# Mask lanes and the first norm in PSUM, two more gathered tiles split into one-pass halves, and 24 row buffers

## The chip, the cores and the metric

The kernel runs on one core of a Trainium2 chip. The metric is the device time of one execution in microseconds (us); lower is better. Times of runs are medians of several executions.

## The reference

Two graph layers over 10,000 nodes of 512 float32 features, and 160,000 edges sorted by destination. What is computed:

```
h   = relu(layernorm(x))
msg = (h @ rel_W[type])[src]                      # one of 4 products for each edge
agg = segment_sum(msg, dst) / max(degree, 1)
x1  = layernorm(h + h @ self_W + agg) * ln1_w + ln1_b
f   = gelu(x1 @ W1 + b1) @ W2 + b2
x   = x + layernorm(x1 + f) * ln2_w + ln2_b
h1  = relu(layernorm(x))
h2  = relu(h1 @ W_self1 + mean_of_neighbours(h1) @ W_neigh1 + b1)
out = x + relu(h2 @ W_self2 + mean_of_neighbours(h2) @ W_neigh2 + b2)
```

## The kernel before

Nodes are handled in 79 blocks: 78 of 128 rows and one of 16, which comes first. The program has four stages: (1) the first norm of the input, the four relation products of every node (written to `hall_d` in DRAM) and the building of edge lists; (2) the fused stage, which gathers and sums messages, and does both layer norms and the feed-forward part; (3) and (4) the two neighbour layers, which gather rows of `h_d`. The change touches stage 2, and through a shared function the order of matmuls in stages 3 and 4.

**Gathering.** `gather` issues indirect DMAs on POOL, each for a tile of 128 rows of 512 floats (L844). A full block has 11 tiles of its own rows (`row`), in which row p of each tile belongs to node p, so that DVE adds them straight into PSUM (`add`, L908). It has five tiles of other edges (`orow`), which PE sums with a 0/1 mask as the stationary operand (`sums`, L897). One more tile is shared by 4 blocks and one by 16 blocks (`srow`). Row tiles come from a ring of buffers, 28 in stage 2 and 56 later, in order of allocation: a gather waits until the last reader of its slot is done.

**Splitting.** In stage 2 the shared tiles are split by `halves_of`: DVE masks off the low 12 bits into `top` (L834, a row tile of the ring), DVE writes the rest to `lower` (L836), and ACT copies `top` to `upper` (L837). Both halves are of type float32r[...].

**Masks.** `hots` builds a block's masks of 128 x 7 x 128 by comparing `lane` with `loc` on DVE (L870). In stages 3 and 4 ACT builds them.

**One iteration of stage 2** handles block b. Instructions of each engine run in program order:

1. DVE builds the mask of block b+1 (L870). In two of four iterations it also adds the feed-forward results of two earlier blocks to their rests and takes their statistics (`second`, L1092, L1063, L1064).
2. DVE adds the block's 11 tiles to PSUM (L908), scales by degree and adds the self product (L1176), and takes statistics.
3. PE runs a part of an earlier group's feed-forward work (`products`): four up products of four matmuls each, with a gelu on ACT after each, or two down products of eight matmuls. A group has four blocks, so the parts go up, up, down, down. One block is turned (transposed) in the middle of a part.
4. ACT takes the square root of the variances, DVE the reciprocal (L1072), and `scaled` applies the norms: ACT scales, DVE multiplies by the weight and adds (L1117, L1118 for the first norm, L1122, L1123 for the second).
5. `begin` gathers for block b+1, splits a shared tile where one starts, and issues the mask matmuls. `products` has issued its last call on PE before them.

The first iterations also multiply 24 late blocks by `self_W`; these pass through tiles of the same ring (`fetch`, `residuals`).

Of the kernel before, what the change touches and what calls it, by code (L numbers as in the profile page):

```python
# [16 lines left out]
P = 128  # L17
# [4 lines left out]
def kernel(  # L22
# [789 lines left out]
    def aligned(ctxa):  # L812

        psA = ctxa.enter_context(tc.tile_pool(name="psA", bufs=2, space=PSUM))
        ring = []
        RINGS = (28, 56)
        UPPER = -(1 << 12)
        rest = list(range(full))
        blocks = ([full] if N % P else []) + rest

# [6 lines left out]
            pool, n = ring[-1]  # L827
            return pool.tile([P, D], F32, name="rows", bufs=n)

        def halves_of(v, lv, pool):  # L830

            top = row_tile()
            hi, lo = (pool.tile([P, D], F32, name=f"{k}{lv}", bufs=1) for k in ("upper", "lower"))
            nc.vector.tensor_scalar(top.bitcast(I32), v.bitcast(I32), UPPER, None,  # L834
                                    op0=OP.bitwise_and)
            nc.vector.tensor_tensor(lo.bitcast(F32R), v, top, op=OP.subtract)  # L836
            nc.scalar.copy(hi.bitcast(F32R), top)  # L837
            return hi, lo

        def gather(b, table, pool, split):  # L840

            def rows(n, idx, name=None, bufs=None):
                t = pool.tile([P, D], F32, name=name, bufs=bufs) if name else row_tile()
                nc.gpsimd.indirect_dma_start(  # L844
                    out=t[:n], out_offset=None, in_=table,
                    in_offset=bass.IndirectOffsetOnAxis(ap=idx, axis=0))
                return t[:n]

            for lv, n in enumerate(SPANS):
                if b < full and b % n == 0:  # L850
                    idx = srow[lv][:, b // n:b // n + 1]
                    if split:
                        tails[lv] = halves_of(rows(P, idx), lv, pool)
                    else:
                        tails[lv] = rows(P, idx, f"tail{lv}", 2)
            others = [rows(P, orow[:, b, t:t + 1]) for t in range(OT if b < full else OT_LAST)]
            if b < full:
                others += tails
            return others, [rows(P, row[:, b, t:t + 1]) for t in range(own(b))]

        def hots(b, pool, scalar=False):
            n = OT + NL if b < full else OT_LAST
            hot = pool.tile([P, OT + NL, P], F32, name="hot", bufs=2)
            if scalar:
# [5 lines left out]
            nc.vector.tensor_tensor(hot[:, :n].bitcast(F32R),  # L870
                                    lane[:, None, :].to_broadcast([P, n, P]),
                                    loc[:, b, :n].unsqueeze(2).to_broadcast([P, n, P]),
                                    op=OP.is_equal)
            return hot
# [6 lines left out]
        def sums(b, others, hot, idle=None):  # L881

            r, n = height(b), len(others)
            pa = psA.tile([P, D], F32, name="pa")
            if idle:
                keep_busy(pa, *idle)
            order = list(range(n)) if b == full else list(range(OT, n))[::-1] + list(range(OT))
            work = []
            for t in order:
                if isinstance(others[t], tuple):  # L890
                    work += [(hot[:, t, :r].bitcast(F32R), v.bitcast(F32R)) for v in others[t]]
                else:
                    work.append((hot[:, t, :r], others[t]))
            if len(work) > n and b % SPANS[0] == 0:
                work = work[-OT:] + work[:-OT]
            for i, (h, v) in enumerate(work):
                nc.tensor.matmul(pa[:r], h, v, start=(i == 0), stop=(i == len(work) - 1))  # L897
            return pa
# [12 lines left out]
        with ExitStack() as s:  # L911
# [1 line left out]
            wp = s.enter_context(tc.tile_pool(name="wp2", bufs=1))  # L913
            gp = s.enter_context(tc.tile_pool(name="gp", bufs=1))
            sp = s.enter_context(tc.tile_pool(name="sp", bufs=3))
            psT = s.enter_context(tc.tile_pool(name="psT2", bufs=2, space=PSUM))
            psH = s.enter_context(tc.tile_pool(name="psH", bufs=2, space=PSUM))
            psO = s.enter_context(tc.tile_pool(name="psO", bufs=2, space=PSUM))
            w1s = wp.tile([P, KC, F], F32, name="w1s")
# [62 lines left out]
            fetch(LATE[0])  # L982
            for b in blocks[:2]:
                load(b)
            first_hot = hots(blocks[0], gp)
# [63 lines left out]
            class Scales:  # L1049
# [27 lines left out]
                def apply(self, out, v, c, r, func):  # L1077
                    nc.scalar.activation(out, v, func, bias=self.rs[:r, 1, c:c + 1],
                                         scale=self.rs[:r, 0, c:c + 1])

            rests = {}
            fed, third = [], []
            now = Scales()
# [13 lines left out]
            def scaled(got, first):  # L1097

                nonlocal third, now
                if first:  # L1100
                    b, c = first
                    r, v = height(b), nodes[b]
                    now.apply(v[:r], v[:r], c, r, AF.Identity)
                if third:
                    h1, at = pair(h1_d, third[0][0], len(third), "h1", 2)
                    for k, (b, c) in enumerate(third):
                        now.apply(h1[:, k, :], xrs.pop(b), c, height(b), AF.Relu)
                    nc.sync.dma_start(at, h1)
                third = []
                for b, v, c in got:  # L1110
                    r = height(b)
                    now.apply(v[:r], v[:r], c, r, AF.Identity)
                if first:
                    b, c = first
                    r, v = height(b), nodes[b]
                    rests[b] = gp.tile([P, D], F32, name="rest", bufs=11)
                    nc.vector.tensor_tensor(rests[b][:r], v[:r], ln1w[:r], op=OP.mult)  # L1117
                    nc.vector.tensor_tensor(rests[b][:r], rests[b][:r], lnb2[:r], op=OP.add)  # L1118
                now = Scales()
                for b, v, c in got:  # L1120
                    r = height(b)
                    nc.vector.tensor_tensor(v[:r], v[:r], ln2w[:r], op=OP.mult)  # L1122
                    nc.vector.tensor_tensor(xrs[b], xrs[b], v[:r], op=OP.add)  # L1123
                    third.append((b, now.stats(xrs[b], r)))
                if got:
                    b, n = got[0][0], len(got)
                    nc.sync.dma_start(rows_of(xn_d, (b, n, height(b))), xrs.pop((b, n)))
# [29 lines left out]
            for bs in plan:  # L1157
                for b in bs:
                    r = height(b)
                    if b == bs[0]:  # L1160
                        before, grp = grp, Group(bs)
                    if i + 2 < len(blocks):
                        load(blocks[i + 2])
                    if i + 1 < len(blocks):
                        hot = hots(blocks[i + 1], gp)
# [24 lines left out]
                    i += 1  # L1190
# [14 lines left out]
        for step, (h_d, ws, wn, bs) in enumerate(((h1_d, ws1, wn1, bs1), (h2_d, ws2, wn2, bs2))):  # L1205
            with ExitStack() as s:
# [45 lines left out]
                    load(i)  # L1252
                turn(blocks[0])
                before = None
                held = begin(blocks[0], hots(blocks[0], ip, True), h_d, ip)
                for i, b in enumerate(blocks):
                    r = height(b)
                    load(i + 3)
                    if i + 1 < len(blocks):
                        hot = hots(blocks[i + 1], ip, True)  # L1260
# [336 lines left out]
```

## Time and profile before

| | us |
|---|---|
| median of 3 runs (lowest to highest) | 6226.65 (6225.09 to 6230.65) |
| the profiled execution's own time | 6229.31 |
| its span, first to last instruction | 6227.6 |
| PE busy (share of the span) | 5669.9 (91%) |
| DVE busy | 3657.2 (59%) |
| ACT busy | 1858.6 (30%) |
| POOL busy | 3769.6 (61%) |
| first to last gather of stage 2 | 1208.0 to 2903.3 |
| first gather of stage 3 | 3002.2 |
| first gather of stage 4 | 4614.2 |

A line of the profile's groups names the source line, engine, operation and tiles (written <- read), the form and the count; then come the busy time in us and the mean of one in ns; then the engine's idle time just before such instructions, and what ended it. "Issue" means that the engine waited for nothing that the profile shows. A float32 matmul stands in the profile as two records.

### The profile page before, as it was taken

What the parts mean: (1) busy time and instruction counts of PE and PEld (TensorE: products, weight loads), DVE (VectorE), ACT (ScalarE), POOL (GpSimd) and SP (SyncE); (2) the same over time, 40 slices, a digit from 0 to 9 for tenths busy, and PEclk for the clock granted to TensorE, in tenths of its full rate; (3) what the DMA queues carried; (4) which work ended last, traced back from release to release, by engine and by line L of the source; (5) the groups of instructions that cost most, each with busy time, mean ns of one, the idle gap of its engine ahead of it and who ended that gap; (6) DMA issues with size and microseconds to landing.
All of it is one profiled execution on the core that took longest, in us unless ns stands there. A gap on an engine that the chain in (4) does not pass through costs nothing.

```text
span 6227.6 us, 55230 instructions
## 1 busy us (share of the span) xinstructions
PE 5669.9 (91%) x15103; PEld 2565.6 (41%) x15103; DVE 3657.2 (59%) x7447; ACT 1858.6 (30%) x3672; POOL 3769.6 (61%) x3927
## 2 busy tenths in 40 slices
PE   9999999899999999999788888888879888888888
PEld 4555554444444444444333333333334333333333
DVE  8889999457777777776333434434434444444444
ACT  1026665023333333333322222222222222222221
POOL 0001110167777777774577777777767777777776
PEclk9999999999999999999899999999999999999999
DMA  4333344487888887885677777777778888888877
GB/s 160 118 126 121 127 138 156 144 276 244 255 252 257 247 252 245 255 255 181 203 237 237 234 237 236 236 237 234 237 232 251 251 247 250 251 247 249 251 246 217
DMA packets 503502, 1373.79 MB, mean 221 GB/s; under 512 B 82206, under 2 KB 82206, under 8 KB 503054
## 3 DMA queue, kind: packets, MB, share of 16 engines
q0 software_dynamic: 308768, 1008.91, 54.4%
q1 hardware_dynamic: 193886, 360.20, 15.9%
q8 instruction: 122, 2.00, 0.1%
q14 instruction: 198, 1.62, 0.1%
q10 hardware_dynamic: 528, 1.05, 0.1%
HBM read 1156.54 MB, written 213.30 MB: 220 GB/s over the span
## 4 chain that ended last, share of the span: by engine, by line
DMA 40%; PE 37%; DVE 9%; issue 7%; POOL 5%; ACT 2%; SPq 0%; POOLq 0%; DVEq 0%; ACTq 0%
DMA rows<-h_d,row 20%; PE pm L774 15%; DMA rows<-h_d,orow 13%; PE pa L897 6%; POOL rows L844 5%; DMA rows<-hall_d,row 5%; PE po L1036 4%; DVE pa L908 4%; PE ph L1025 4%; PE pm L678 2%; PE po L1268 1%; PE po L976 1%; DMA rows<-hall_d,orow 1%; DVE st L1063 1%; PE pT L172 1%
## 5 line engine op out<-in xcount | busy, mean ns | idle before, releaser
L908 DVE TENSOR_TENSOR pa<-pa,rows 128x512 f32<-128x512 f32 x2574 | 1799.2, 699 | 2061.9 <-PE pa L897 1212.3
L844 POOL DMA_INDIRECT rows<-h_d,row x1716 | 1622.3, 945 | 522.7 <-issue 285.7
L897 PE MATMUL pa<-rows,hot 128*128 128x512 f32 (+1 forms) x2358 | 1240.4, 639 | 375.9 <-DMA rows<-h_d,orow 321.1
L844 POOL DMA_INDIRECT rows<-hall_d,row x858 | 870.1, 1014 | 268.7 <-issue 111.2
L844 POOL DMA_INDIRECT rows<-h_d,orow x786 | 743.1, 945 | 354.9 <-issue 102.0
L897 PEld LDWEIGHTS pa<-rows,hot 128*128 128x128 f32 (+1 forms) x2358 | 399.7, 192 | 1156.7 <-DMA rows<-h_d,orow 830.1
L844 POOL DMA_INDIRECT rows<-hall_d,orow x393 | 377.4, 960 | 350.5 <-PE pm L678 203.4
L1268 PE MATMUL po<-wss,hTb 128*128 128x512 f32 (+1 forms) x1264 | 588.7, 610 | 0.0
L1036 PE MATMUL po<-w2s,hid 128*128 128x512 f32 (+1 forms) x1264 | 564.4, 600 | 16.7 <-DVE rest L1092 13.5
L1239 PE MATMUL po<-wns,mTb 128*128 128x512 f32 (+1 forms) x1264 | 574.3, 597 | 1.4 <-ACT mTb L173 1.4
L1025 PE MATMUL ph<-x1T,w1s 128*128 128x512 f32 (+2 forms) x1344 | 558.9, 569 | 4.8 <-ACT hid L1027 4.8
L173 ACT COPY mTb<-pT 128x512 f32<-128x512 f32 (+1 forms) x158 | 91.9, 581 | 1231.7 <-PE pT L172 1231.7
L1264 ACT ACTIVATE mb<-pa,rdeg 128x512 f32<-128x512 f32 (+1 forms) x158 | 108.6, 687 | 1131.9 <-DVE pa L908 1128.6
L879 PE MATMUL pa<-wss,ident 128*128 128x512 f32 x936 | 427.5, 593 | 0.0
L513 POOL DMA_INDIRECT win<-rec_d,at x79 | 81.4, 1031 | 528.4 <-PE pe L538 348.0
L1239 PEld LDWEIGHTS po<-wns,mTb 128*128 128x128 f32 (+1 forms) x1264 | 240.5, 191 | 308.5 <-issue 272.8
L1025 PEld LDWEIGHTS ph<-x1T,w1s 128*128 128x128 f32 x1344 | 249.7, 192 | 282.0 <-issue 272.9
L1036 PEld LDWEIGHTS po<-w2s,hid 128*128 128x128 f32 (+1 forms) x1264 | 237.0, 191 | 306.3 <-issue 281.8
L897 PE MATMUL pa<-tail,hot 128*128 128x512 f32 x624 | 307.8, 610 | 48.9 <-DMA tail<-h_d,srow 48.7
L866 ACT ACTIVATE hot<-lane,loc 128x128 f32<-128x128 f32 x1098 | 337.7, 390 | 0.0
L1268 PEld LDWEIGHTS po<-wss,hTb 128*128 128x128 f32 (+1 forms) x1264 | 237.2, 198 | 241.4 <-issue 241.0
L774 PE MATMUL pm<-wrel,hT 128*128 128x512 f32 x624 | 296.5, 597 | 0.0
(304 smaller groups left out, 6344.3 us busy)
## 6 DMA issues: line engine op xcount, KB each, us to landing
hall_d<-p SPq DMA_DIRECT2D x156, 256.0 KB, 2.5
hall_d<-u SPq DMA_DIRECT2D x156, 256.0 KB, 2.5
hb<-h_d SPq DMA_DIRECT2D x156, 256.0 KB, 4.2
rows<-h_d,row POOLq DMA_INDIRECT x1716, 3.8
xg<-in_x_dram SPq DMA_DIRECT2D x39, 512.0 KB, 3.8
xr_d<-xg SPq DMA_DIRECT2D x39, 512.0 KB, 2.8
xs<-xs_d SPq DMA_DIRECT2D x39, 512.0 KB, 6.6
h_d<-h SPq DMA_DIRECT2D x39, 512.0 KB, 4.6
```

The lines of the kernel that those rows point to most:

```text
L678: nc.tensor.matmul(pm, a[:, k, :], w[:, k, :], start=(k == 0), stop=(k == KH - 1))
L774: nc.tensor.matmul(pm, a[:, k, :], w[:, k, :], start=(k == 0), stop=(k == KH - 1))
L844: nc.gpsimd.indirect_dma_start(out=t[:n], out_offset=None, in_=table, in_offset=bass.IndirectOffsetOnAxis(ap=idx, axis=0))
L866: nc.scalar.activation(hot[:, t, :], lane, AF.Abs, bias=loc[:, b, t:t + 1], scale=-1.0)
L879: nc.tensor.matmul(p, ident, w, start=True, stop=True)
L897: nc.tensor.matmul(pa[:r], h, v, start=(i == 0), stop=(i == len(work) - 1))
L908: nc.vector.tensor_tensor(pa[:r], pa[:r], t[:r], op=OP.add)
L1025: nc.tensor.matmul(ph[:, :n], w1s[:, k, f * P:(f + 1) * P], self.xT[:, k, :n], start=(k == 0), stop=(k == KC - 1))
L1036: nc.tensor.matmul(po[:r], self.hid[:, f, c * r:(c + 1) * r], w2s[:, f, :], start=(f == 0), stop=(f == FC - 1))
L1239: nc.tensor.matmul(po[:r], mT[:, k, :r], wns[:, k, :], start=False, stop=(k == KC - 1))
L1264: nc.scalar.activation(m[:r], pa[:r], AF.Copy, scale=rdeg[:r, b:b + 1])
L1268: nc.tensor.matmul(po[:r], hT[:, k, :r], wss[:, k, :], start=(k == 0), stop=False)
```

## The change

- `hots` in stage 2 reads the lane numbers from a PSUM copy (`lanes`), made once by ACT. Stages 3 and 4 keep their masks on ACT; the flag `scalar` becomes the absence of `lanes`.
- The block's sum stays in PSUM: the step at L1176 writes `pa` in place instead of `xs`, the statistics read `pa`, ACT's scaled copy goes from `pa` to `xs`, and the first norm's rest is made from `pa` by `affine`.
- `affine` replaces a scaling on ACT, a multiply and an add by two scalar-tensor-tensor operations on DVE: subtract the mean and multiply by the weight in place, then multiply by the reciprocal deviation and add. It is used for the first norm's rest and for the second norm. The second norm is now done before the first norm's rest.
- The first two of a block's five `orow` tiles are split by `halves_of`. Their `top` tiles come from the ring as well.
- In a full block the five `orow` tiles are multiplied from last to first, in all stages, so that the split ones come last. Where a shared tile starts, the three unsplit tiles come first, then the shared halves, then the two split tiles.
- The ring of stage 2 has 24 row tiles, not 28. The transposes have one PSUM buffer, not two; the lanes take the other bank.

```diff
-        RINGS = (28, 56)
+        RINGS = (24, 56)
+        SPLIT = 2
...
             others = [rows(P, orow[:, b, t:t + 1]) for t in range(OT if b < full else OT_LAST)]
+            if split and b < full:
+                for t in range(SPLIT):
+                    others[t] = halves_of(others[t], NL + t, pool)
...
             nc.vector.tensor_tensor(hot[:, :n].bitcast(F32R),
-                                    lane[:, None, :].to_broadcast([P, n, P]),
+                                    lanes[:, None, :].to_broadcast([P, n, P]),
...
-            order = list(range(n)) if b == full else list(range(OT, n))[::-1] + list(range(OT))
+            order = list(range(n)) if b == full else list(range(OT, n))[::-1] + list(range(OT))[::-1]
...
-            if len(work) > n and b % SPANS[0] == 0:
-                work = work[-OT:] + work[:-OT]
+            if b < full and isinstance(others[OT], tuple) and b % SPANS[0] == 0:
+                work = work[2 * NL:2 * NL + OT - SPLIT] + work[:2 * NL] + work[2 * NL + OT - SPLIT:]
...
-            psT = s.enter_context(tc.tile_pool(name="psT2", bufs=2, space=PSUM))
+            psT = s.enter_context(tc.tile_pool(name="psT2", bufs=1, space=PSUM))
+            psC = s.enter_context(tc.tile_pool(name="psC", bufs=1, space=PSUM))
...
+            lanes = psC.tile([P, D], F32, name="lanes")[:, :P]
+            nc.scalar.copy(lanes, lane)
+            first_hot = hots(blocks[0], gp, lanes)
...
+                def affine(self, out, v, c, r, w, to):
+                    nc.vector.scalar_tensor_tensor(v, v, self.mv[:r, c, 0:1], w[:r],
+                                                   op0=OP.subtract, op1=OP.mult)
+                    nc.vector.scalar_tensor_tensor(out, v, self.rs[:r, 0, c:c + 1], to,
+                                                   op0=OP.mult, op1=OP.add)
...
-                    now.apply(v[:r], v[:r], c, r, AF.Identity)
+                    now.apply(nodes[b][:r], pa[:r], c, r, AF.Identity)
...
+                last, now = now, Scales()
                 for b, v, c in got:
                     r = height(b)
-                    now.apply(v[:r], v[:r], c, r, AF.Identity)
+                    last.affine(xrs[b], v[:r], c, r, ln2w, xrs[b])
+                    third.append((b, now.stats(xrs[b], r)))
                 if first:
...
-                    nc.vector.tensor_tensor(rests[b][:r], v[:r], ln1w[:r], op=OP.mult)
-                    nc.vector.tensor_tensor(rests[b][:r], rests[b][:r], lnb2[:r], op=OP.add)
-                now = Scales()
-                for b, v, c in got:
-                    r = height(b)
-                    nc.vector.tensor_tensor(v[:r], v[:r], ln2w[:r], op=OP.mult)
-                    nc.vector.tensor_tensor(xrs[b], xrs[b], v[:r], op=OP.add)
-                    third.append((b, now.stats(xrs[b], r)))
+                    last.affine(rests[b][:r], pa[:r], c, r, ln1w, lnb2[:r])
...
-                    nc.vector.scalar_tensor_tensor(v[:r], pa[:r], rdeg[:r, b:b + 1], v[:r],
+                    nc.vector.scalar_tensor_tensor(pa[:r], pa[:r], rdeg[:r, b:b + 1], v[:r],
                                                    op0=OP.mult, op1=OP.add)
-                    first = (b, now.stats(v[:r], r))
+                    first = (b, now.stats(pa[:r], r), pa)
```

More of the change, by code (lines that the diff above doesn't have):

```diff
@@ L828, in row_tile, with halves_of @@
             return pool.tile([P, D], F32, name="rows", bufs=n)
-        def halves_of(v, lv, pool):
+        def halves_of(v, lv, pool, bufs=1):
             top = row_tile()
-            hi, lo = (pool.tile([P, D], F32, name=f"{k}{lv}", bufs=1) for k in ("upper", "lower"))
+            hi, lo = (pool.tile([P, D], F32, name=f"{k}{lv}", bufs=bufs) for k in ("upper", "lower"))
             nc.vector.tensor_scalar(top.bitcast(I32), v.bitcast(I32), UPPER, None,
@@ L859, in gather, with hots @@
             return others, [rows(P, row[:, b, t:t + 1]) for t in range(own(b))]
-        def hots(b, pool, scalar=False):
+        def hots(b, pool, lanes=None):
             n = OT + NL if b < full else OT_LAST
             hot = pool.tile([P, OT + NL, P], F32, name="hot", bufs=2)
-            if scalar:
+            if lanes is None:
                 for t in range(n):
@@ L984, in aligned @@
                 load(b)
-            first_hot = hots(blocks[0], gp)
+            lanes = psC.tile([P, D], F32, name="lanes")[:, :P]
+            nc.scalar.copy(lanes, lane)
+            first_hot = hots(blocks[0], gp, lanes)
             residuals(LATE[0])
@@ L1100, in scaled @@
                 if first:
-                    b, c = first
-                    r, v = height(b), nodes[b]
-                    now.apply(v[:r], v[:r], c, r, AF.Identity)
+                    b, c, pa = first
+                    r = height(b)
+                    now.apply(nodes[b][:r], pa[:r], c, r, AF.Identity)
                 if third:
@@ L1109, in scaled @@
                 third = []
+                last, now = now, Scales()
                 for b, v, c in got:
                     r = height(b)
-                    now.apply(v[:r], v[:r], c, r, AF.Identity)
+                    last.affine(xrs[b], v[:r], c, r, ln2w, xrs[b])
+                    third.append((b, now.stats(xrs[b], r)))
                 if first:
-                    b, c = first
-                    r, v = height(b), nodes[b]
+                    b, c, pa = first
+                    r = height(b)
                     rests[b] = gp.tile([P, D], F32, name="rest", bufs=11)
-                    nc.vector.tensor_tensor(rests[b][:r], v[:r], ln1w[:r], op=OP.mult)
-                    nc.vector.tensor_tensor(rests[b][:r], rests[b][:r], lnb2[:r], op=OP.add)
-                now = Scales()
-                for b, v, c in got:
-                    r = height(b)
-                    nc.vector.tensor_tensor(v[:r], v[:r], ln2w[:r], op=OP.mult)
-                    nc.vector.tensor_tensor(xrs[b], xrs[b], v[:r], op=OP.add)
-                    third.append((b, now.stats(xrs[b], r)))
+                    last.affine(rests[b][:r], pa[:r], c, r, ln1w, lnb2[:r])
                 if got:
@@ L1164, in aligned @@
                     if i + 1 < len(blocks):
-                        hot = hots(blocks[i + 1], gp)
+                        hot = hots(blocks[i + 1], gp, lanes)
                     ready = []
@@ L1254, in aligned @@
                 before = None
-                held = begin(blocks[0], hots(blocks[0], ip, True), h_d, ip)
+                held = begin(blocks[0], hots(blocks[0], ip), h_d, ip)
                 for i, b in enumerate(blocks):
@@ L1259, in aligned @@
                     if i + 1 < len(blocks):
-                        hot = hots(blocks[i + 1], ip, True)
+                        hot = hots(blocks[i + 1], ip)
                     pa, mine = held
```

## Prediction

> **What bounds the kernel now.** I read the page's busy shares first, then its costliest groups, then the fused stage alone. PE is busy 91% of the span and POOL only 61%, but the groups of the gathers (L844; busy us, mean ns of one, idle before) show another picture:
>
> ```profile
> L844 POOL DMA_INDIRECT rows<-h_d,row x1716 | 1622.3, 945 | 522.7 <-issue 285.7
> L844 POOL DMA_INDIRECT rows<-hall_d,row x858 | 870.1, 1014 | 268.7 <-issue 111.2
> ```
>
> 268.7 us over 858 gathers is 0.31 us before each, and so it is in the last two stages (522.7/1716 = 0.30). The timelines show this gap after nearly every gather: it is the pace of issue, not a wait. So a gather costs POOL 0.945 + 0.304 = 1.249 us, and that queue is full. Next, the steady part of the fused stage (1400 to 2900 us):
>
> ```profile
> L844 POOL DMA_INDIRECT rows<-hall_d,row x779 | 793.5, 1019 | 237.3 <-issue 100.5 <-DMA rows<-hall_d,row 40.8 <-DMA rows<-hall_d,orow 27.1
> L844 POOL DMA_INDIRECT rows<-hall_d,orow x351 | 335.9, 957 | 106.9 <-issue 30.5 <-DVE pa L908 25.6 <-DMA rows<-hall_d,row 22.5
> ```
>
> 1152 gathers with their gaps take 1149 + 351 = 1500 us of 1500: POOL bounds this stage. A block has 16.32 gathers, so 70.6 blocks pass, 21.25 us each: 16.32 x 1.249 = 20.38, and 0.88 of lengthening ((1019-945) x 779 + (957-945) x 351 = 61.9 us). The two timelines side by side (start, duration) show what lengthens them:
>
> ```profile
> 1979.16 1.19 POOL L844 DMA_INDIRECT rows<-hall_d,row  x1 [0.30 <-DMA rows<-hall_d,orow]
> 1983.49 1.21 POOL L844 DMA_INDIRECT rows<-hall_d,row  x1 [0.30 <-DVE mv L1064]
> 1986.26 1.09 POOL L844 DMA_INDIRECT rows<-hall_d,row  x1 [0.30 <-DMA rows<-hall_d,row]
> ```
> ```profile
> 1978.84 0.69 DVE L1117 TENSOR_TENSOR rest<-xs,ln1w 128x512 f32<-128x512 f32 x1 [0.88 <-ACT xs L1078]
> 1983.23 0.66 DVE L1122 TENSOR_TENSOR rest<-rest,ln2w 128x512 f32<-128x512 f32 x1
> 1985.48 1.06 DVE L870 TENSOR_TENSOR hot<-lane,loc 128x896 fp32r<-128x896 f32 x1
> ```
>
> Each long gather ends 0.82 us after the end of a DVE operation that was running 0.13 us after the gather began (1985.48 + 1.06 + 0.82 = 1987.36; 1986.26 + 1.09 = 1987.35). Tallying all such pairs of the stage, the lengthening ends with L870 29.9 us, L1123 11.2, L1118 9.2, L1117 7.3, L1122 6.9, the halves 0.5; never with L908, L1176 or L1063. DVE's waits say how far behind it stands:
>
> ```profile
> DVE pa L908 <- DMA rows<-hall_d,row: 155.4, 148, 4.0
> DVE rs L1072 <- ACT rs L1070: 80.8, 71, 3.3
> DVE rest L1117 <- ACT xs L1078: 63.5, 72, 0.9
> ```
>
> 155.4 us over 71 blocks: 2.2 us a block in which DVE waits for rows. That is all its slack.
>
> **What the Trainium skill says.** "SBUF — State Buffer", section Who interferes with whom: a DVE instruction with two SBUF inputs, or in a two-port mode, shuts out a GpSimd instruction that reads SBUF; with one SBUF input and no such mode it doesn't. The tally agrees, except that a gather is caught at one point only, not over its length. "FP8 and Floating Point Precision", TensorE Precision Notes: true fp32 takes four passes. Here an fp32 tile takes PE 0.86 us (ten records from 2042.76 to 2047.05) and each half 0.23 (2042.06, 2042.29, 2042.52). "TensorE: Matmul & The Clock Gate", Part 1: an idle window of some 3.4 us halves PE's clock. The page's clock row dips only to 0.8-0.9; the longest fp32 record, 1223 ns against 592, fits.
>
> **The change part by part** (per block; 78 full blocks).
>
> 1. *Lanes, first norm in PSUM.* L870, L1117 and L1118 keep one SBUF input. Their 46.4 us of lengthening go: -0.60. The second norm still has two SBUF inputs: its 18.1 us (0.23) stay.
> 2. *Two split tiles, on POOL.* Each adds one L834 (0.42 us, one source, SBUF to SBUF) and one L836 (0.69, two SBUF inputs), back to back: 2.2 us of shutting out. A gather is caught every 1.25 us. Entering in the first 0.42 us (chance 0.34) it waits 0.21 on average, and the next gather, 1.25 after that release, is caught in the fourth operation for 0.64; entering in the second operation (0.55) it waits 0.35. Together 0.5. Bounds: 0 if hidden behind an earlier catch (the 25 pairs of the shared tiles cost 0.5 us in all, following L1118 directly, which no longer shields them), 1.0 if always met. So POOL: 20.38 + 0.88 - 0.60 + 0.50 = 21.16 (20.7 to 21.7), a change of about -0.1.
> 3. *On DVE.* Two pairs, 0.45 + 0.65 each with overlap: +2.2. Scalar-tensor-tensor took 0.75 with a pointer scalar (L1176) and 0.69 without (L1244), so the four replacements cost 0 to 0.06 each: +0.2 in second-norm iterations, +0.1 in the others. In iterations with a second norm that work now runs ahead of the first norm and covers the 0.88 wait for ACT; the 0.65 wait of L1122 for ACT falls where there was one.
> 4. *The cycle.* From mask build to mask build, less row waits, DVE's timeline has four kinds in turn: 21.3 and 22.0 (with second norm), 15.1 and 16.3 (without). They become 22.8, 22.9, 17.4, 18.6. The last two are now under PE's own cycle: products 13.9 (2027.55 to 2041.43), then 1.3 for the shared halves, 3 x 0.86 and about 1.1 for the new halves: 18.9. The sum is 22.8 + 22.9 + 18.9 + 18.9 = 83.5, or 20.9 a block.
> 5. *The new wait.* PE's queue holds the two split tiles last in each sum, and products behind them; both halves need DVE's L834 and ACT's cast, which come after the second norm. With second norm PE waits some 22.8 - 18.9 = 4 us there. That is longer than the clock window: half a window's work is lost, up to 1.7 us. ACT's square root stands behind the gelu of the third up product, and DVE waits for it; so a late PE makes DVE late in the iterations with up products, one of each kind: (0 to 1.7) x 2/4 = 0 to 0.9, taken as 0.6. Hence 21.5 a block against POOL's 21.16: the loop DVE-PE-ACT becomes the bound. +0.25 x 78 = +20.
> 6. *Ring of 24.* Tops take two more slots: 18.6 a block, not 16.6. A slot comes round after 24/18.6 = 1.3 blocks, 27 us; a row gathered at 2020.6 was added at 2029.9 to 2030.6, 10 us later, in the slowest iteration 12. Even 4 us more leave over 10: nothing in steady state. At the start late tiles fill it too: POOL stood still for 24.4 us until the shared halves were made (L837, gather at 1265.19). In the changed order three gathers more wait for those, 3 x 1.25, and two more pairs are ahead: +4 (0 to 10).
> 7. *Reversed tile order*, in the last two stages too. PE starts fp32 tiles when the fifth has landed, and ends the sum 3.3 us later (4.3 against 1.0 after that landing). Adds then end at 4.3 + 8.1 = 12.4 us after it, still before the last row (11 x 1.25 = 13.8). POOL hides it: 0. If one idle stretch in place of five halves the clock, PE's 17 us a block grow to at most 20.4 against 20.2: at worst +0.2 x 158 = +30. I take +6.
> 8. One transpose buffer (used once in 21 us, read out in 1.5), one ACT copy, fewer ACT scalings (ACT is 35% busy there): 0. DMA bytes are unchanged.
>
> Sum: +20 + 4 + 6 = +30. The profiled run took 6229.3 us (span 6227.6), 2.7 over the median of the runs: 6229 + 30 = 6259, and as a median 6257.
>
> **The rivals.**
> - *POOL's relief wins* (faster, 0.24). DVE's 2.2 us of slack covers the 2.0 it gains, PE's wait costs nothing (20.9 a block), and the halves catch few gathers (0.1 to 0.3, POOL 20.8 to 21.0). Then -0.25 to -0.45 x 78: -20 to -35, or 6195 to 6215 with the start. It decides as long as the loop's mean stays under some 21.0. For it: POOL is the proven bound. Against it: the slack is an average, and the iterations with second norm have none (eleven adds back to back, 8.01 us from 2052.22).
> - *An even trade* (within 0.2%, 0.14). The halves give back what lanes and norm save (-0.60, +0.50), and the loop stays under POOL: 6220 to 6238.
> - *The DVE-PE-ACT loop* (forecast, 0.50): 6240 to 6285. It decides once its mean passes 21.25 a block, with 0.35 us of PE delay carried over.
> - *Worse still* (0.12): the clock loss is whole in every iteration and in the last stages, or POOL itself waits for ring slots, 1 us a block = 78 us: 6285 to 6330. Against it: reuse leaves 10 us.
>
> **The numbers.** A measurement of this kernel tells 0.2%, some 12 us, from no change. Faster 0.24, same 0.14, slower 0.62. For 8 in 10 the range reaches into the first and last rivals: 6203 to 6308.
>
> **What would show it.** Steady windows: period 21.4 to 21.6; DVE busy from 16.0 to over 18 a block; its wait for rows from 155 us to under 60; PE waiting over 1 us a block for upper or lower; no gather lengthened by the mask build or the first norm, but some by the new pairs. Wrong, if row waits stay above 100 us with a shorter period, if gathers begin to idle over 0.3 us, or if the last two stages move by over 10 us.

## The result and the profile after

The changed kernel takes 6282.25 us (median of 6 runs, 6280.03 to 6283.49), the kernel before 6229.32 in the same comparison (6 runs, 6225.09 to 6232.53). The ratio is 1.0085, 95% interval 1.0072 to 1.0098: slower by 53 us, where +30 was forecast.

| profiled execution, us | before | after | difference |
|---|---|---|---|
| own time | 6229.31 | 6283.11 | +53.8 |
| first gather of stage 2 | 1208.0 | 1207.0 | -1.0 |
| last gather of stage 2 | 2902.4 | 2946.5 | +44.1 |
| first gather of stage 3 | 3002.2 | 3059.7 | +57.5 |
| from there to the end | 3225.4 | 3221.7 | -3.7 |
| period of stage 2 (mask build to mask build, blocks 7 to 75) | 21.02 | 21.85 | +0.83 |

All of the loss lies in the fused stage. The gathers' groups of the whole page (busy us, mean ns of one, idle before):

```profile
L845 POOL DMA_INDIRECT rows<-h_d,row x1716 | 1622.9, 946 | 522.7 <-issue 261.4
L845 POOL DMA_INDIRECT rows<-hall_d,row x858 | 821.5, 957 | 330.0 <-issue 115.1
```

In stages 3 and 4 the gathers are as before. In stage 2 a gather of own rows now takes 957 ns and not 1014, but 330.0 us of idle time stand before them and not 268.7. The same groups in the steady part alone, 1400 to 2900 us:

```profile
L845 POOL DMA_INDIRECT rows<-hall_d,row x756 | 724.1, 958 | 266.2 <-issue 101.7 <-DVE pa L912 38.4 <-DMA rows<-hall_d,row 32.0
L845 POOL DMA_INDIRECT rows<-hall_d,orow x344 | 337.6, 981 | 146.5 <-PE pa L901 46.3 <-issue 45.7 <-DVE rows L835 16.8
```

With the shared tiles 1121 gathers were made where 1152 were before. A gather of own rows takes less than before (958 ns, not 1019), one of other edges more (981, not 957), and all of them together 0.964 us on average, not 0.998. POOL is faster at its work and waits between the gathers: it has stopped being the bound. Two pairs of the timelines (start, duration) show the relief, POOL first, then what DVE did:

```profile
2011.68 1.15 POOL L845 DMA_INDIRECT rows<-hall_d,row  x1 [0.30 <-issue]
...
2014.38 0.94 POOL L845 DMA_INDIRECT rows<-hall_d,row  x1 [0.30 <-issue]
```
```profile
2011.59 0.42 DVE L835 TENSOR_SCALAR rows<-rows 128x512 int32<-128x512 int32 x1
...
2013.78 1.08 DVE L874 TENSOR_TENSOR hot<-lanes,loc 128x896 fp32r<-128x896 f32 x1
```

The mask build (L874) ran all through the start of the second gather and no longer holds it: 0.94 us. The first gather was caught by a mask-off of the new halves and ends 0.82 us after that one's end (2011.59 + 0.42 + 0.82 = 2012.83), the rule found in the profile before. Tallied over stage 2, the lengthening fell from 65.1 us to 23.0: the mask build from 29.9 to none, the first norm from 16.5 to 0.2, the second norm from 18.1 to 14.7, the halves up from 0.5 to 8.2.

What DVE waits for between 1400 and 2900 us has turned over:

```profile
DVE rs L1079 <- ACT rs L1077: 130.7, 68, 5.4
DVE pa L912 <- PE pa L901: 31.6, 35, 1.1
DVE pa L1090 <- ACT xs L1085: 28.8, 34, 0.8
```

The 155.4 us of waits for rows are gone; the wait of the reciprocal for ACT's square root grew from 80.8 to 130.7 us. Two more waits, in the lists of PE and of POOL, were small before (11.6 us for the upper halves, 3.0 us for PE's sums):

```profile
PE pa L901 <- ACT upper L838: 145.6, 52, 4.5
```
```profile
POOL rows L845 <- PE pa L901: 70.7, 40, 4.6
```

PE waits 2.1 us a block for the upper halves (145.6 over 68.7 blocks), and POOL for slots of its ring, whose last reader is PE. One iteration with up products and a second norm shows how these hang together: PE's timeline, then ACT's, then DVE's (the last column is the idle time before, and its releaser):

```profile
2164.01 0.79 PE L901 MATMUL pa<-upper,hot 128*128 128x512 f32 x1 [3.16 <-ACT upper L838]
...
2165.88 9.03 PE L1032 MATMUL ph<-x1T,w1s 128*128 128x512 f32 x16
...
2175.18 7.03 PE L1032 MATMUL ph<-x1T,w1s 128*128 128x512 f32 x16
```
```profile
2178.82 0.69 ACT L1034 ACTIVATE hid<-ph,b1s 128x512 f32<-128x512 f32 x1 [1.78 <-PE ph L1032]
2179.52 1.28 ACT L1077 ACT_TABLE_LOAD   x1
2180.82 0.30 ACT L1077 ACTIVATE rs<-mv,eps 128x5 f32<-128x5 f32 x1
```
```profile
2177.59 0.18 DVE L1071 BATCH_NORM_AGGREGATE mv<-st 128x2 f32<-128x6 f32 x1
2181.15 0.19 DVE L1079 RECIPROCAL rs<-rs 128x5 f32<-128x5 f32 x1 [3.38 <-ACT rs L1077]
```

PE stood 3.16 us for a half, then ran its first up products at half rate (9.03 us for sixteen records, where the next sixteen took 7.03: some five records of 0.86 us instead of 0.43). Hence the third gelu, at 2178.82, came late, and the square root, queued behind it and a table load, later. DVE had its statistics at 2177.77 and stood for 3.38 us. It is late with its next work, the halves of the following block among it, and so PE is late again. On this reading the loop closes; the experiments below test it.

By kind of iteration (mean in us, mask build to mask build; DVE's busy time, durations summed with their overlaps, and its wait at L1079 within it):

| kind | forecast | after | DVE busy | wait for square root |
|---|---|---|---|---|
| down products, second norm | 22.8 | 23.1 | 22.5 | 0.36 |
| up products, second norm | 22.9 | 24.4 | 21.8 | 2.29 |
| up products | 18.9 | 21.6 | 14.7 | 4.67 |
| down products | 18.9 | 18.3 | 16.0 | 0.36 |
| mean | 20.9, with carried delay 21.5 | 21.85 | 18.8 | 1.92 |

### The profile page after: what moved, and what is told of

The parts are those of the page before. It is cut to its first block, busy times and chain, and to the rows that moved or that the text cites. A ratio compares the mean times of both kernels' runs of the same rounds, so it can differ in the third digit from the quotient of the medians.

```text
span 6281.4 us, 55663 instructions
## 1 busy us (share of the span) xinstructions
PE 5630.6 (90%) x15103; PEld 2673.9 (43%) x15103; DVE 3845.1 (61%) x7759; ACT 1892.9 (30%) x3750; POOL 3728.8 (59%) x3927
## 4 chain that ended last, share of the span: by engine, by line
PE 45%; DMA 25%; DVE 18%; issue 5%; POOL 4%; ACT 3%; POOLq 0%; SPq 0%; DVEq 0%; ACTq 0%
PE pm L774 15%; DMA rows<-h_d,orow 13%; PE pa L901 13%; DMA rows<-h_d,row 10%; DVE pa L912 8%; PE ph L1032 7%; POOL rows L845 4%; PE pm L678 2%; PE po L1248 2%; DVE st L1070 2%; PE po L1043 2%; PE po L1277 2%; DVE lower L837 1%; PE po L981 1%; PE pa L883 1%
## 5 line engine op out<-in xcount | busy, mean ns | idle before, releaser
L912 DVE TENSOR_TENSOR pa<-pa,rows 128x512 f32<-128x512 f32 x2574 | 1798.8, 699 | 1921.0 <-PE pa L901 1739.7
L901 PE MATMUL pa<-rows,hot 128*128 128x512 f32 (+1 forms) x2046 | 1102.2, 691 | 397.5 <-DMA rows<-h_d,orow 393.6
L845 POOL DMA_INDIRECT rows<-hall_d,row x858 | 821.5, 957 | 330.0 <-issue 115.1
L901 PEld LDWEIGHTS pa<-rows,hot 128*128 128x128 f32 (+1 forms) x2046 | 441.2, 222 | 1014.6 <-DMA rows<-h_d,orow 494.1
L1032 PE MATMUL ph<-x1T,w1s 128*128 128x512 f32 (+2 forms) x1344 | 602.4, 604 | 2.6 <-ACT hid L1034 2.6
L173 ACT COPY mTb<-pT 128x512 f32<-128x512 f32 (+1 forms) x158 | 91.9, 582 | 1657.1 <-PE pT L172 1657.1
L1277 PE MATMUL po<-wss,hTb 128*128 128x512 f32 (+1 forms) x1264 | 568.8, 593 | 0.0
L1032 PEld LDWEIGHTS ph<-x1T,w1s 128*128 128x128 f32 x1344 | 271.3, 208 | 295.5 <-issue 283.1
L901 PE MATMUL pa<-upper,hot 128*128 128x512 f32 x312 | 176.4, 566 | 151.4 <-ACT upper L838 151.3
L901 PE MATMUL pa<-tail,hot 128*128 128x512 f32 x624 | 293.8, 593 | 6.6 <-DMA tail<-h_d,srow 4.9
```

The lines of the kernel that those rows point to most:

```text
L845: nc.gpsimd.indirect_dma_start(out=t[:n], out_offset=None, in_=table, in_offset=bass.IndirectOffsetOnAxis(ap=idx, axis=0))
L912: nc.vector.tensor_tensor(pa[:r], pa[:r], t[:r], op=OP.add)
L1032: nc.tensor.matmul(ph[:, :n], w1s[:, k, f * P:(f + 1) * P], self.xT[:, k, :n], start=(k == 0), stop=(k == KC - 1))
L1277: nc.tensor.matmul(po[:r], hT[:, k, :r], wss[:, k, :], start=(k == 0), stop=False)
```

## Experiments

The chips of the first eight runs (e and f) were slower in stages 2 to 4 whatever the kernel, 7057 and 7067 us for the kernel before, so those are read as ratios to the kernel before on the same chip; the last four (g) ran where it takes 6224. "Early" below is one edit: ACT is given the square root after the second of four up products instead of after the third. The norms' scalings that follow the root move with it, so that all of them come ahead of the turn of one block and of the third gelu. With down products nothing changes.

```diff
                 for i, call in enumerate(work):
-                    if i == len(work) - 1:
+                    if i == len(work) // 2:
                         yield
```

My theory: the halves make PE late, and a late PE makes DVE late only because the square root stands behind the third gelu. Rivals: the halves' own work on DVE and PE is the price; PE's half clock is; the ring of 24 is.

| run | what it is | ratio to before | 95% interval |
|---|---|---|---|
| e1_nosplit | changed, no split `orow` tile | 0.9976 | 0.9958 to 0.9993 |
| e2_split1 | changed, one split tile | 1.0066 | 1.0044 to 1.0087 |
| e3_sqrt_early | changed, early | 0.9962 | 0.9950 to 0.9973 |
| e4_warm | changed, idle matmuls | 1.0190 | 1.0152 to 1.0227 |
| f1_after | changed | 1.0167 | 1.0139 to 1.0194 |
| f2_sqrt_early | changed, early | 0.9921 | 0.9896 to 0.9946 |
| f3_nosplit | changed, no split `orow` tile | 0.9994 | 0.9977 to 1.0011 |
| f4_nosplit_early | no split `orow` tile, early | 0.9955 | 0.9928 to 0.9982 |
| g1_before | before, for its profile | one run: 6225.1 us | |
| g2_before_sqrt | before, early | 1.0007 | 0.9999 to 1.0016 |
| g3_split_only | before, split tiles, their order, ring of 24 | 1.0155 | 1.0141 to 1.0169 |
| g4_early_fwd | changed, early; forward order in stages 3, 4 | 0.9994 | 0.9986 to 1.0002 |

### How many tiles are split: e1, e2

```diff
-        SPLIT = 2
+        SPLIT = 0      # e1 (and f3); e2: SPLIT = 1
```

> The changed kernel with no split orow tiles (SPLIT = 0); lanes, first norm, affine, tile order and ring of 24 as changed. If the loop of DVE, PE and ACT with the new halves costs the time, this one is bound by POOL again: 16.32 gathers x 1.249 us = 20.4 a block plus 0.25 of lengthening, some 20.65 against 21.2 before and 21.85 after, so 85 to 100 us under the changed kernel and 30 to 45 under the one before (6185 to 6200). If the smaller ring or the reversed tile order cost it, it stays within 15 us of the changed kernel.

> One split tile in place of two. Loop theory: DVE loses one pair (1.1 us) in every iteration and PE waits less; the loop comes to about 20.6 a block, level with POOL, so 6190 to 6225: near the unsplit kernel, not half way. If each split tile costs a fixed amount on POOL (a caught gather or a ring slot), half of the difference between two and none remains.

Without split tiles the loss is gone (0.9976), with one it is 1.0066, and with two, on the other slow chip, 1.0167: about 0.01 of the time for each tile. The loss comes with the halves. What of them costs it, these two don't tell. One split tile was expected near none and came out half way, as the reading with a fixed cost a tile had it; g4 below, which keeps both tiles without a loss, speaks against such a fixed cost.

### The square root's place, and PE's clock: e3, e4

e3 is "early" on the changed kernel. e4 puts three idle fp32 matmuls ahead of the sum in iterations with a second norm:

```diff
-                        held = begin(blocks[i + 1], hot, table, gp, split=True)
+                        held = begin(blocks[i + 1], hot, table, gp,
+                                     idle=(w1s[:, 0, :D], 3) if got else None, split=True)
```

> The changed kernel with the square root issued after the second up product, not the third, so that ACT has two gelus ahead of it. Chain theory (PE late, third gelu late, square root late, DVE late): DVE's wait for the root (2.3 and 4.7 us in the two kinds of iteration with up products) falls to under 2 in both, 1.0 to 1.4 us a block on average less, the mean below 21.0 where POOL takes over: 6190 to 6225. If DVE's work alone is the loop, under 10 us are gained.

> The changed kernel with three dummy matmuls (2.6 us) ahead of the mask sum in iterations with a second norm, where PE waits 3 to 4 us for the halves; nothing else is changed and the result is not touched. If the halved clock after that wait is part of the cost, the first up products after it take 7.0 us instead of up to 9.0, and 0.5 to 1 us a block goes: 6205 to 6245. If the clock is only a symptom, the time stays within 10 us of the changed kernel, and it gets worse if PE's own work is short of time.

With the square root early the changed kernel is faster than the kernel before on that chip (0.9962). e4 gained nothing against the changed kernel (1.0190 there, 1.0167 on the other slow chip). It doesn't settle what the clock costs, since the idle matmuls ran in the wrong place, as its PE timeline shows:

```profile
2050.85 2.74 PE L883 MATMUL pa<-w1s,ident 128*128 128x512 f32 x6
...
2054.35 2.74 PE L901 MATMUL pa<-rows,hot 128*128 128x512 f32 x6
2066.84 0.80 PE L901 MATMUL pa<-upper,hot 128*128 128x512 f32 x1 [9.75 <-ACT upper L838]
...
2068.71 8.49 PE L1032 MATMUL ph<-x1T,w1s 128*128 128x512 f32 x16
```

They came before the sum's own products. The wait behind those stayed (9.75 us), and the up products after it again took 8.49 us.

### Halves against square root, two by two: f1 to f4

> The changed kernel itself, beside the kernel before on this chip, so that the next three runs can be set against it. Expected as measured: 1.0085 of the kernel before. On a chip where every stage stalls more (the first four experiments ran on one with 7057 us for the kernel before) POOL is not full, and the loss may be less: 1.002 to 1.010.

> As the changed kernel, but the second norm's square root is given to ScalarE in the middle of the products of the other edges instead of one product before their end, so that it comes ahead of the last casts of halves and of the third gelu. My theory (the square root behind gelu and casts is what the halves cost: L1079 waited 130.7 us for L1077 between 1400 and 2900 us of the changed kernel's trace, 1.9 us a block): L1079's waits fall to under 0.6 us a block, the period from 21.85 to about 20.9, and the time by 0.010 to 0.012 of the kernel before, against the run of the changed kernel beside it. Rival (the halves' added VectorE work of 2.2 us a block and PE's waits for them are the cost, the square root only the place where it shows): the wait moves to L912, and the time falls by less than 0.004.

> Lanes and first norm in PSUM, ring of 24, but no tile of the other edges is split (SPLIT = 0): their products are five full fp32 ones again. My theory: POOL's lengthened gathers go as in the changed kernel (65 us before, 25 after; about 17 now), worth 0.5 us a block, and the rows are waited for by DVE as before: 0.993 to 0.999 of the kernel before, so the halves alone cost 0.010 to 0.015. Rival (the loss comes from lanes, the Identity op's place or the ring of 24, not from the halves): 1.004 to 1.010.

> No splitting, and the square root in the middle of the products: both edits together. If the halves' loss is the square root's queue alone, this and the early square root with halves give nearly the same time, both limited by POOL's gathers: 0.988 to 0.996. If the halves cost VectorE and PE time besides, this is faster than the early square root with halves by over 0.003. If an early square root only puts the gelu off, this is slower than without splitting alone.

(The "products of the other edges" in the text on f2 should read: the feed-forward's up products; the edit is the one shown above.)

All four ran on one chip. f1 came out at 1.0167 where 1.0085, or 1.002 to 1.010, was expected. "Early" takes 0.0246 from the kernel with split tiles, about twice what was expected, and 0.0039 from the one without, where the two intervals overlap. DVE's waits of the changed kernel (f1), then of the same with "early" (f2), 1400 to 2900 us:

```profile
DVE rs L1079 <- ACT rs L1077: 222.7, 41, 10.5
```
```profile
DVE pa L912 <- PE pa L901: 126.6, 28, 12.0
...
DVE rs L1079 <- ACT rs L1077: 18.8, 25, 9.3
```

The wait for the square root falls from 222.7 to 18.8 us. Part of it moves to L912, as the rival said, but the time falls 0.025, not under 0.004: the queue is what costs. The size of the wait alone doesn't tell its price, though: without split tiles it falls too, from 210.7 (f3) to 91.9 us (f4), and little is gained. The changed kernel's loss there is twice that on the first chip, and this wait is longer too (222.7 us against 130.7); why isn't shown. f3 came out at no difference where 0.993 to 0.999 was expected: POOL isn't full there (448.5 us of idle time before 669 gathers of own rows, 0.67 us each and not 0.30), so there is little that its relief could speed up. f2 against f4, 0.9921 to 0.9955, has overlapping intervals, so whether the halves help once the square root is early stays open.

### On the chip where the kernel before takes 6224 us: g1 to g4

> The kernel before, for its profile on a chip like that of the experiments (7057 to 7067 us there, 6229 where it was first profiled). My reading is that engines stand still there in all of stages 2 to 4 for reasons outside the program: then the fused stage's period is about 24.5 us instead of 21.0, POOL is no longer full, and DVE's wait for ScalarE's square root (L1072 for L1070: 80.8 us in the first profile, 1.1 us a block) is clearly longer, 2 to 4 us a block, though less than the changed kernel's 4.4 us a block (f1_after). If the added time lay in stages 3 and 4 alone, the period would be 21 to 22 us.

> The kernel before with one edit: the square root is given to ScalarE after the second of four up products instead of after the third. The changed kernel gained 0.0246 from this edit (1.0167 to 0.9921 on one chip), the kernel without split tiles 0.0039 (0.9994 to 0.9955). My theory (the halves make PE late, and only a late PE makes the third gelu, and the square root behind it, late): the kernel before, which has no split tiles, gains about what the unsplit one did, 0.993 to 0.998. Rival (the square root's place is worth the same with any kernel, and the changed kernel's parts have nothing to do with it): 0.970 to 0.982.

> The kernel before with the split tiles, the order of tiles and the ring of 24, but lanes and first norm left in SBUF. My theory (halves alone make the loss; lanes and first norm in PSUM relieve POOL, which is not full on this chip): 1.010 to 1.020, about the changed kernel's 1.0167. Rival (the loss needs the second norm's place ahead of the first norm, or the first norm's affine form): 0.998 to 1.006.

> The changed kernel with the early square root, and with the reversed order of the five tiles only in stage 2, where tiles are split; stages 3 and 4 multiply them first to last as before. Against the early square root alone (0.9921): if the reversed order makes PE idle in one piece before each sum in stages 3 and 4 and costs half-rate clock (my +6 us), this is faster by 0.001 or more; if it lets PE start its sum only when the last tile has landed and DVE's adds end later for it, the same; if, as the trace of the changed kernel has it (stages 3 and 4 took 3.7 us less than before), it does no harm: 0.990 to 0.994, no difference that can be told.

g1 was meant for a slow chip and ran on one like the first: its period is 20.97 us, and its waits are those of the first profile (rows 152.8 us, square root 79.4). It says nothing on the slow chips, but it makes g2 to g4 comparable with the profiles of before and after.

g2, "early" on the kernel before, makes no difference: 1.0007, outside both expectations. Its wait at L1072 hardly moved, from 79.4 to 75.4 us. ACT's and DVE's waits of g2, and the table load in the profile before, show why:

```profile
ACT L1070 <- DVE mv L1064: 330.1, 36, 14.8
```
```profile
DVE rs L1072 <- ACT rs L1070: 75.4, 71, 2.0
```
```profile
2020.56 1.28 ACT L1070 ACT_TABLE_LOAD   x1 [16.38 <-DVE mv L1064]
```

In every second iteration the table load itself waits for DVE's statistics, and the root comes 1.28 us after them, wherever the gelus stand: the wait at L1072 is 1.7 to 1.8 us in the kinds without a second norm, in g1 and in g2. PE hardly waited for halves there (11.6 us in the profile before), so "early" had no delay to take away. POOL was full besides (0.305 us of idle time before each of 780 gathers of own rows). In all versions with split tiles the load no longer waits, and the wait with down products is 0.36 us (after); why the load has moved isn't shown.

g3 leaves the lanes and the first norm in SBUF and is worse than the whole change, 1.0155 against 1.0085 on the first comparison. Its DVE waits:

```profile
DVE rs L1076 <- ACT rs L1074: 134.0, 67, 5.3
DVE rest L1121 <- ACT xs L1082: 59.1, 67, 0.9
```

The square root's wait is as long as with the whole change (2.0 us a block); the second line is the wait of the first norm's rest for ACT in every iteration; in the whole change half of it is covered (28.8 us). The lengthening is back at 71.2 us. So the halves, with their order and the ring of 24, cost some 96 us (0.0155 of 6224), and the rest of the change gives some 44 back (0.0155 less 0.0085, from two comparisons).

g4 is the changed kernel with "early", and with the forward order where no tile is split. It takes 6219.45 us, no difference from before (0.9994, where 0.990 to 0.994 was expected), and so all 53 us of the loss are gone. The forward order has no part in that: stages 3 and 4 took 3224.6 us with it, 3221.7 without. Its DVE waits, 1400 to 2900 us, and the same kind of iteration as above on PE, ACT and DVE (this kernel's lines stand one lower):

```profile
DVE pa L913 <- PE pa L902: 66.9, 35, 3.5
DVE rs L1080 <- ACT rs L1078: 34.7, 71, 1.5
DVE pa L1091 <- ACT xs L1086: 30.5, 36, 0.8
```
```profile
2131.56 0.50 PE L902 MATMUL pa<-upper,hot 128*128 128x512 f32 x1 [3.49 <-ACT upper L838]
...
2132.59 8.73 PE L1033 MATMUL ph<-x1T,w1s 128*128 128x512 f32 x16
```
```profile
2141.36 0.69 ACT L1035 ACTIVATE hid<-ph,b1s 128x512 f32<-128x512 f32 x1 [2.75 <-PE ph L1033]
2142.06 1.28 ACT L1078 ACT_TABLE_LOAD   x1
2145.36 0.30 ACT L1078 ACTIVATE rs<-mv,eps 128x5 f32<-128x5 f32 x1 [2.01 <-DVE mv L1072]
...
2151.00 1.26 ACT L1035 ACTIVATE hid<-ph,b1s 128x512 f32<-128x512 f32 x2
```
```profile
2145.14 0.18 DVE L1072 BATCH_NORM_AGGREGATE mv<-st 128x2 f32<-128x6 f32 x1
2145.69 0.19 DVE L1080 RECIPROCAL rs<-rs 128x5 f32<-128x5 f32 x1 [0.37 <-ACT rs L1078]
```

In this kind of iteration PE is as late as before (3.49 us of waiting, 8.73 us for the up products), and DVE does not wait for it. ACT loads its table after the second gelu and now waits for DVE, 2.01 us, where DVE waited 3.38 for it. This is the case's plainest proof: the same late PE, the same halves, the same ring, another place in ACT's queue, and 63 us less (6282.25 less 6219.45; the two medians are from two comparisons whose kernels before differ by 5.5 us). So neither the halves' work nor the half rate of PE nor the ring of 24 makes the loss without that place. POOL is nearly full again:

```profile
L845 POOL DMA_INDIRECT rows<-hall_d,row x781 | 749.8, 960 | 247.0 <-issue 82.5 <-DMA rows<-hall_d,row 53.3 <-DVE pa L913 26.8
L845 POOL DMA_INDIRECT rows<-hall_d,orow x352 | 349.4, 993 | 107.2 <-issue 32.9 <-DVE rows L835 15.5 <-DVE pa L1091 9.7
```

From 1400 to 2860 us a gather of stage 2 came every 1.283 us in g4, every 1.300 in g1, every 1.337 after. But g4 isn't faster than before: its last gather of stage 2 comes at 2880.0, 17.6 us ahead of g1's, and the first of stage 3 only 4.1 us ahead (2994.2 against 2998.3). Its mean period is 20.96 us, that of g1 20.97, but the two come about differently. In the kernel before, POOL starts with a lead: from a block's last gather to DVE's last add it is 21 us in block 4 and 4 to 7 us from block 16 on. Blocks 8 to 24 live on it at 20.5 us each; after them a block takes POOL's 21.2. In g4 this time is 8 to 17 us at first and 15 to 20 from block 28 on, and by blocks 56 to 72 it is POOL that waits for the loop, 0.3 us a block, and a block takes 21.1 us. With a second norm DVE is full (busy 22.6 of 23.2 and 22.1 of 22.8 us). POOL ends further ahead, and the drain after the last gather is longer for that, 114.2 us against 100.7. The relief of POOL is real and has little to speed up.

No version tried beats both kernels where the kernel before takes 6224 us. On the slow chips the versions with "early" do (e3 0.9962, f2 0.9921, f4 0.9955). Unsplit tiles with lanes and first norm in PSUM were not run on a chip of the first kind, with or without "early".

## Why the prediction was right, and where it was short

Right in direction and mechanism: the loop of DVE, PE and ACT took over from POOL, as forecast, by a late PE and a square root behind the third gelu. +30 us was too little by 23. That it was no further off is in part luck: two terms were short by some 36 us together, two others too high by 14.

1. *Lanes and first norm, -0.60 a block on POOL:* right. 46.4 us of lengthening became 0.2.
2. *Halves on POOL, +0.50:* too much. They ended 8.2 us of lengthening against 0.5 before, 0.1 a block. Part of the reason can be read from the trace: some of the halves' operations gave way themselves. Of 181 mask-offs 67 took over 0.04 us longer than the shortest (0.42), up to 0.62; 66 of these had begun 0.58 to 0.72 us after a gather and ended some 1.19 us after its start. With step 1, POOL got more relief than forecast. The rival "POOL's relief wins" was right on this, and wrong that it would decide.
3. *DVE, +2.2 and +0.1 to +0.2:* right. It was busy 1132.91 us of the stretch before (16.0 a block) and 1255.61 after (18.3 a block).
4. *The four kinds, 20.9 a block without carried delay:* near. In g4, where the square root hardly passes delay on (its wait is 0.5 us a block), the loop sets the pace in blocks 56 to 72, at 21.1. In the changed kernel the kinds with down products took 41.4 us together (41.7 forecast), those with up products 46.0 (41.8 forecast).
5. *Delay carried through the square root, "0 to 0.9, taken as 0.6":* the term that was too small. PE's wait was about right (4 us forecast after each second norm; 3.1 and 4.0 measured after the two kinds, 2.1 a block in all). The loss of clock was larger than "up to 1.7": 2.0 us in the up products of the iteration shown, besides the halves ahead of them, which ran at half rate too (635 ns a record of the up products on average, 592 before). And only the loss of clock was taken as carried over; PE's wait and the place behind the third gelu, with a table load after it, were not added. The wait at L1079 beyond its floor of 0.36 us was 1.93 and 4.31 us in the two kinds with up products, 1.6 us a block, and the mean period came out 0.95 above 20.9, not 0.6. Over the 68 blocks from 7 to 75 that is 24 us.
   A second term of the sum was off: the loop's 21.5 was set against POOL's 21.25. DVE's own period in the kernel before was 21.02 between blocks 7 and 75, while POOL's gathers passed at 1.303 us each, 21.27 a block of 16.32: DVE was using up the lead that POOL had at the start (21 us in block 4, 4 to 7 from block 16 on). That is another 0.23 x 68 = 16 us.
6. *Ring of 24, 0 in steady state and +4 at the start:* POOL did wait for slots (70.7 us), which the forecast counted as a sign of the worse rival. g4, with the same ring, shows 13.8 us of it: it followed from the late loop. The cost of the ring itself wasn't measured alone. At the start the changed kernel was level, not 4 us behind (mask build of block 7 at 1381.5 us, 1381.6 before).
7. *Reversed order, +6:* wrong in sign. Stages 3 and 4 took 3221.7 us (after) and 3222.8 (g3) with it, and 3225.4, 3225.0, 3224.0 and 3224.6 (before, g1, g2, g4) without: about -2.5 us.
8. *The rest, 0:* nothing contradicts it.

One sign of being wrong came true although the mechanism held: gathers idle over 0.3 us (0.35 before those of own rows, 0.43 before those of other edges). A loop that outlasts POOL makes POOL wait, so this sign could not tell the forecast from its failure.

The account of the miss of 23, by the mask builds: from block 7 to 75 the changed kernel lost 56 us where 20 was forecast, +36 (the +24 and +16 of step 5, less 3 for the ten blocks outside this stretch that the 20 counts); -4 at the start (step 6); +1.5 between block 75 and stage 3; -10 in stages 3 and 4 (step 7): together some +24.

## What to carry to other kernels

When one engine is relieved, look for the loop that comes next, and in it for the instruction that another engine waits for although it needs nothing of what stands ahead of it in its queue. Such a place cost nothing while no engine ahead of it was late (g2), and carried a third engine's delay into the loop once one was. What it costs when the third engine is late and something else is the bound wasn't tried. Moving the square root, with the scalings behind it, ahead in a queue gave back all that the change had lost here; and what a relieved engine gains is worth something only down to the next loop's period.

## What the runs showed of the hardware

- Of a gather and a DVE operation that meet, either may be the longer for it, by the point at which they meet. The Trainium skill, "SBUF — State Buffer", Who interferes with whom, calls the port pair that DVE and GpSimd share an exclusive lock; here a gather lost up to 0.27 us in the lines shown (1.21 against 0.945), and a mask-off of 0.42 us up to 0.2.
- The Trainium skill, "ScalarE: Activation LUTs", What ACT_TABLE_LOAD costs, states 1283 ns for the load and 2.66 us with a drain. Here the load took 1.28 us; the gelu ahead of it ended 0.01 us before it began (2178.82 + 0.69, 2179.52), and the square root began 0.02 us after it. No drain shows.
- Of PE's 34 waits of 3.16 us and more for halves in the changed kernel (1300 to 2950 us) 33 were followed by half rate (fp32 records 0.85 us apart, not 0.43), which lasted until 2.7 to 6.1 us after the wait; of 17 waits of 1.1 us none was. So somewhat less than the 3.4 us of the prediction was enough.
- Two chips ran the same kernel 13% slower (7057 and 7067 us against 6224). Stage 1 ended at the same time on all chips (first gather of stage 2 at 1206.0 to 1208.6 us in every run), and stages 3 and 4 took 3772 to 3800 us instead of 3222 to 3225. There the engines often stand for 10 to 20 us with nothing that the profile shows as releaser. What it is stays open.
